# An MLP cut by inner width instead of by tokens, in a four-layer Mamba/FFT/convolution kernel

## The chip, the cores and the metric

The kernel runs on one core of one Trainium2 chip, in float32. The metric is the device time of one execution in microseconds (us); a lower one is better. A core has five engines that run side by side, each with its own queue of instructions: TensorE (PE in the profile; its weight loads are listed as PEld), VectorE (DVE), ScalarE (ACT), GpSimd (POOL) and SyncE (SP), which here issues all the DMAs.

## The reference, cut to what matters

The input is 8 images of 384 channels and 32 x 32 pixels, so 1024 tokens an image. Four layers follow each other, each added to its input: layer 0 is a Mamba block (inner width 768, 16 states), layer 1 an 8 x 8 patch FFT filter with a depthwise convolution and a gate, layer 2 a Mamba block with a layer norm ahead and an MLP behind, layer 3 a 3 x 3 depthwise convolution. The change touches only the MLP of layer 2:

```
# t: tokens x 384, the output of layer 2's Mamba block
t = gelu(t @ mlp_w1.T + mlp_b1, approximate=False) @ mlp_w2.T + mlp_b2
# mlp_w1: 1536 x 384, mlp_w2: 384 x 1536
x = x + t
```

## The kernel before, in words

Channels lie on the 128 partitions (KC = 3 blocks of 128), tokens on the free axis. An image is worked in NCH = 2 chunks of T = 512 tokens. Layers 0 and 1 run for all images first, then layers 2 and 3, joined by the intermediate x_mid in DRAM. So there are 16 chunks of layer 0 and 16 chunks of layer 2.

The backbone is the scan. A chunk has NQ = 24 steps. In a step t the program (the loop at line 1015) issues: the product with B on POOL for the next step (`times`, L623), the four scans on DVE (`scan`, L643, with two products with C on DVE, L654, and one on POOL, L660), filler, the reduction of the step before on TensorE (`gather`, the y matmuls), the load of the g tile three steps ahead (`begin`, L613), more filler, and the matmuls and exponentials of the next step's decay (`decay`, the dA matmuls and L241). The four dA banks of PSUM are single, so the dA matmuls of step t+1 come after DVE has read those of step t, and after all filler that stands ahead of them in TensorE's queue.

The filler is everything else: the projections in (ps_in) and of the gates (ps_z), the output projection (ps_out), the MLP (ps_up, ps_dn), layer 3 (ps_dw), norms and loads. Each is a Python generator, a job, which yields after each piece. `Jobs` hands out pieces while the step has room: it counts a matmul as its columns over 600 units and gives a step of layer 2 a room of 6.4 units of TensorE and 3.0 of VectorE (`ROOM`). A piece is let in when the remaining room is at least what the piece of the same number needed in the last job of its kind. Jobs go in the order of their due step `last`; unused room is carried over up to an eighth, and debt is carried over in full. `jobs.until` forces pieces without regard to room when a step needs their result. A job that yields NEXT goes on in the next step, one that yields EARLY at the start of the next step. `pipe` runs units of several stages through PSUM banks (`NBANK` = 3); with `deep=1` one unit at a time, one stage a piece, and the last stage of a unit shares its piece with the first of the next.

The MLP belongs to the job `finish(s)`: `out_proj` writes t into SBUF (three tiles of 128 x 512) and calls `weights()`; then `mlp(s)` runs. It goes over two halves of the tokens (TH = 256). In each half the up stage makes all NF = 12 blocks of the inner width: for a pair of blocks f, f+1 it takes one weight tile (128 x 6 x 128, 384 KB), puts 2 x 3 matmuls of 256 columns into the two halves of one bank, and ACT evicts the two halves with the bias into h1 (128 x 12 x 256). Then two gelus over 1536 columns each, then the down stage: for each of the 3 output blocks m two weight tiles and 12 matmuls of 256 columns, all 12 accumulated in PSUM, and one scalar_tensor_tensor on DVE that adds the sum and the bias b2 to x.

The weight tiles (tag mw) have 4 buffers. `weights()` lists the 12 tiles twice, once a half, and asks for the first four. `take()` asks for one more tile (`more()`, L889, on SP's queue) and hands out the oldest loaded. The request goes into the buffer of the tile just used up, so it waits for TensorE's last matmul of that tile. On SP's queue stand also the g loads (L613, 1 MB each, which wait for the y matmuls to free a buffer) and the spills of du (L590, four for each d, which wait for POOL).

A float32 matmul of the program is two TensorE instructions, each with a weight load, in the profile: 72 up matmuls a chunk x 16 chunks are 2304 instructions. All matmuls are issued on line 177, all activations on line 241; the tiles tell them apart.

Of the kernel before, what the change touches and what calls it, by code (L numbers as in the profile page):

```python
# [10 lines left out]
F32 = mybir.dt.float32  # L11
AF = mybir.ActivationFunctionType
ALU = mybir.AluOpType
# [3 lines left out]
P = 128  # L17
B, C, H, W = 8, 384, 32, 32
L = H * W
KC = C // P  # L20
# [6 lines left out]
T = 512  # L27
NCH = L // T
FF = 4 * C
NF = FF // P  # L30
# [23 lines left out]
def _flat(ap):  # L54
    return ap.rearrange("p a b -> p (a b)")
# [100 lines left out]
def tile_conv_preact_d4(ctx: ExitStack, tc: tile.TileContext, a: dict, out: bass.AP):  # L156
# [13 lines left out]
    vector = Meter(nc.vector, work, 1)  # L170

    def mm(out_, lhsT, rhs, start=True, stop=True):
        columns = 1
        for n in rhs.shape[1:]:
            columns *= n
        work[0] += columns / 600
        nc.tensor.matmul(out_, lhsT, rhs, start=start, stop=stop)  # L177
# [11 lines left out]
    def pipe(units, deep=2):  # L189


        flying = []
        units = deque(units)
        while units or flying:
            went = bool(flying)
            for f in list(flying):
                if f["stages"]:
                    f["stages"].popleft()(f["ps"])
                settle(f)
                if not f["stages"]:  # L200
                    flying.remove(f)
            if units and live["ps"] < NBANK and len(flying) < deep:
                went = True
                name, stages = units.popleft()
                live["ps"] += 1
                ps = psg.tile([P, 512], F32, tag="ps", name=name)
                stages[0](ps)
                f = {"stages": deque(stages[1:]), "ps": ps, "bank": True}
                settle(f)
                if f["stages"]:  # L210
                    flying.append(f)
            if units or flying:
                yield None if went else WAIT

    def settle(f):
        if f["bank"] and (not f["stages"] or f["stages"][0] is None):
            f["bank"] = False
            ps_done()
            if f["stages"]:
                f["stages"].popleft()  # L220

    def both(*stages):


        def run(ps):
            for stage in stages:
                stage(ps)

        return run
# [3 lines left out]
    def act(out_, in_, func, **kw):  # L233

        if func in (AF.Exp, AF.Ln):
            if act_set["now"] != "exp":
                nc.scalar.preload_act_table_set(SET_EXP)
                act_set["now"] = "exp"
        elif func not in (AF.Identity, AF.Copy, AF.Square, AF.Abs):
            act_set["now"] = func  # L240
        nc.scalar.activation(out_, in_, func, **kw)  # L241

    def exp_again():

        nc.scalar.preload_act_table_set(SET_EXP)
        act_set["now"] = "exp"

    def rsqrt(out_, in_, eps):
# [20 lines left out]
    ln_w, ln_b, b1, b2 = (  # L269
        vec2[:, 0:3], vec2[:, 3:6], vec2[:, 6 : 6 + NF], vec2[:, 18:21],  # L270
    )
# [414 lines left out]
    def out_proj(s):  # L686
# [6 lines left out]
        if last:  # L693
            while "done" not in chunks[B * NCH - 1]:
                yield WAIT
            if p2 is None:
                open_p2()
            s["weights"] = weights()
            s["t"] = [p2.tile([P, T], F32, tag="t", name="t", bufs=3) for _ in range(KC)]
# [22 lines left out]
    def finish(s):  # L722

        yield from out_proj(s)
        t = NQ * s["n"]
        if s["n"] == B * NCH - 1:
            load_out(layer_w["l2_"], "l2_")
        if s["pre"] == "l2_":
            yield from mlp(s)
        s["ended"] = True  # L730
        if s["pre"] == "l2_":
            if s["c"] == NCH - 1:
                jobs.add("layer3", layer3(s), 0, t + 3 * NQ - 1)
        elif s["c"] == NCH - 1:
            until = 2 * NQ + 3 if s["n"] == B * NCH - 1 else 3 * NQ - 2
            jobs.add("layer1", layer1(s), 0, t + until)

    p2 = None
# [120 lines left out]
        s["done"] = True  # L859


    TH = T // 2
    NFH = NF // 2
    xp = None

# [6 lines left out]

    def weights():

        parts = [a["l2_mlp_w1"][f : f + 2].rearrange("f p k q -> p f k q") for f in range(0, NF, 2)]
        parts += [
            a["l2_mlp_w2"][m][:, g * NFH : (g + 1) * NFH, :]
            for m in range(KC)
            for g in range(2)
        ]  # L880
        parts = deque(parts + parts)
        loaded = deque()

        def more():
            if parts:
                w = p2.tile([P, NFH, P], F32, tag="mw", name="mw", bufs=4)
                part = parts.popleft()
                to = w if len(part.shape) == 3 else w.rearrange("p (f k) q -> p f k q", f=2)
                nc.sync.dma_start(to, part)  # L889
                loaded.append(w)  # L890

        for _ in range(4):
            more()
        return loaded, more

    def mlp(s):
        x = s["x"]
        loaded, more = s["weights"]
        first = True

        def take():

            nonlocal first
            if not first:
                more()
            first = False
            return loaded.popleft()

        for half in range(2):
            cols = slice(half * TH, (half + 1) * TH)  # L910
            h1 = p2.tile([P, NF, TH], F32, tag="h1", name="h1")

            def up(f):
                def run(q):
                    def run_q(ps):
                        if q == 0:
                            now[0] = take()
                        cols_q = slice(q * TH, (q + 1) * TH)
                        for k in range(KC):
                            mm(  # L920
                                ps[:, cols_q], now[0][:, q * KC + k, :],
                                s["t"][k][:, cols], start=k == 0, stop=k == KC - 1,
                            )

                    return run_q

                def evict(ps):
                    for q in range(2):
                        act(
                            h1[:, f + q, :], ps[:, q * TH : (q + 1) * TH], AF.Identity,  # L930
                            bias=b1[:, f + q : f + q + 1],
                        )

                now = [None]
                return [run(0), both(run(1), evict)]

            yield from pipe([("ps_up", up(f)) for f in range(0, NF, 2)], deep=1)
            yield EARLY
            for q in range(2):
                part = _flat(h1[:, q * NFH : (q + 1) * NFH, :])  # L940
                act(part, part, AF.Gelu)
            exp_again()
            yield NEXT

            def down(m):
                def sum_up(g, third):
                    def run(ps):
                        if third == 0:
                            now[0] = take()
                        for f in range(third * KC, (third + 1) * KC):  # L950
                            mm(
                                ps[:, :TH], now[0][:, f, :], h1[:, g * NFH + f, :],
                                start=g == 0 and f == 0, stop=g == 1 and f == NFH - 1,
                            )

                    return run

                now = [None]

                def add(ps):  # L960
                    xc = x[:, m, cols]
                    vector.scalar_tensor_tensor(
                        xc, ps[:, :TH], b2[:, m : m + 1], xc, ALU.add, ALU.add
                    )

                return [sum_up(0, 0), sum_up(0, 1), sum_up(1, 0), both(sum_up(1, 1), add)]

            yield from pipe([("ps_dn", down(m)) for m in range(KC)], deep=1)

    def layer3(s):  # L970
# [44 lines left out]
    for t in range(total):  # L1015
        s, i = steps[t]
# [16 lines left out]
        if t > 0:  # L1033
            p, q = steps[t - 1]
# [4 lines left out]
        if t + AHEAD < total:  # L1039
            p, q = steps[t + AHEAD]  # L1040
# [138 lines left out]
```

## Time and profile before

| | |
|---|---|
| three runs | 7766.74, 7783.18, 7798.79 us; median 7783.18 |
| profiled execution | 7774.96 us; span 7773.2 us; 1.8 us around it |
| mean granted TensorE clock | 0.922 |
| scans of layer 2 with their filler | about 4068 to 7600 us |
| tail without scans (last out projection, MLP, layer 3) | about 7600 to 7773 us |
| mw loads | 384 of 384 KB; 7.4 us from issue to landing in the median, 16.2 at most |
| all DMA | 1122.5 MB, 144 GB/s over the span |

The groups of instructions that the change touches (count, busy us, mean ns of one):

| group | count | busy us | mean ns |
|---|---|---|---|
| PE ps_up, 256 columns | 2304 | 566.8 | 394 |
| PE ps_dn, 256 columns | 2304 | 573.9 | 401 |
| ACT eviction h<-ps_up, 128 x 256 | 384 | 158.4 | 474 |
| ACT gelu of h, 128 x 1536 | 64 | 91.4 | 1476 |
| DVE x<-ps_dn, 128 x 256 | 96 | 45.3 | 472 |

How to read it: the mean of a matmul is its own length from first to last column out; matmuls of a group overlap, so their pace is read from starts in the timeline, not from the mean. "idle before, releaser" is the time an engine stood still ahead of an instruction, and the event that ended it. SPq is SP's queue of DMAs.

### The profile page before, as it was taken

The page shows a single profiled execution, that of the slowest core. Times are in us where ns is not written, and L with a number is a line of the kernel's source. Part 1 is how long each engine was busy: PE and PEld are TensorE (multiplying, and loading weights), DVE is VectorE, ACT ScalarE, POOL GpSimd, SP SyncE. Part 2 cuts the span into 40 slices and gives each one's busy share as a digit, 9 for nine tenths or more (in the row PEclk, how much of TensorE's full clock was granted, in tenths as well). Part 3 has the DMA queues.
Part 4 walks back from the last instruction along what each step waited for, and adds up shares of the span by engine and source line. Part 5 has one row for each costly group of instructions (what it writes and reads, how often), then busy time and mean ns, then how long its engine had stood idle before and what let it go on. Part 6 is the DMA issues. An engine that isn't in the chain of part 4 may idle for free. (4 is left out here: it accounts for less than half of the span.)

```text
span 7773.2 us, 76689 instructions
## 1 busy us (share of the span) xinstructions
PE 7244.1 (93%) x25762; PEld 3001.0 (39%) x25762; DVE 5787.0 (74%) x7350; ACT 4034.0 (52%) x6980; POOL 5638.8 (73%) x2710
## 2 busy tenths in 40 slices
PE   7989999999999999999999989999999999999998
PEld 2223333333333333333334434444444444444445
DVE  5988788888777878778746765767777677776871
ACT  4445555554554555455545544555555555555543
POOL 5888878788787878778646764767767677676770
PEclk8888889999888999988899999999999999999999
DMA  5666556556565646556536654666656666565662
GB/s 141 141 151 144 138 134 142 136 135 150 127 146 127 141 120 148 128 139 146 129 78 167 174 135 120 165 156 172 165 150 174 155 170 164 149 164 146 171 168 67
DMA packets 288919, 1122.50 MB, mean 144 GB/s; under 512 B 37386, under 2 KB 90970, under 8 KB 190220
## 3 DMA queue, kind: packets, MB, share of 16 engines
q1 hardware_dynamic: 288524, 1117.59, 58.4%
q8 instruction: 204, 3.34, 0.2%
q14 instruction: 191, 1.56, 0.1%
HBM read 1041.96 MB, written 75.50 MB: 144 GB/s over the span
## 5 line engine op out<-in xcount | busy, mean ns | idle before, releaser
L623 POOL TENSOR_TENSOR g<-g,bc 128x1024 f32<-128x1024 f32 x1536 | 3586.8, 2358 | 197.2 <-DMA g<-dud 181.2
L660 POOL TENSOR_TENSOR g<-g,bc 128x1024 f32<-128x1024 f32 x768 | 1806.2, 2352 | 1441.1 <-DVE carry L656 806.6
L241 ACT ACTIVATE dA<-dA,w_A 128x512 f32<-128x512 f32 x3072 | 1860.7, 662 | 1543.3 <-PE dA L177 1530.1
L177 PE MATMUL dA<-dt,selr 32*128 32x512 f32 x6144 | 1573.3, 677 | 70.6 <-DVE g L654 61.9
L643 DVE TENSOR_TENSOR_SCAN dA<-dA,carry,g 128x512 f32<-128x512 f32 x768 | 986.6, 1285 | 616.0 <-issue 275.6
L643 DVE TENSOR_TENSOR_SCAN dA<-dA,g 128x512 f32<-128x512 f32 x768 | 940.6, 1225 | 477.5 <-issue 167.7
L654 DVE TENSOR_TENSOR g<-dA,bc 128x512 f32<-128x512 f32 x1536 | 1053.9, 686 | 29.8 <-DVE dA L643 0.5
L177 PE MATMUL y<-g,sely 128*32 128x512 f32 x6144 | 934.1, 637 | 43.0 <-POOL g L660 37.5
L643 DVE TENSOR_TENSOR_SCAN g<-dA,carry,g 128x512 f32<-128x512 f32 x768 | 940.6, 1267 | 0.0
L643 DVE TENSOR_TENSOR_SCAN g<-dA,g 128x512 f32<-128x512 f32 x768 | 893.3, 1204 | 0.0
L177 PEld LDWEIGHTS dA<-dt,selr 32*128 32x128 f32 x6144 | 470.2, 191 | 984.4 <-DVE g L643 517.3
L177 PE MATMUL ps_dn<-h,mw 128*128 128x256 f32 x2304 | 573.9, 401 | 75.3 <-DMA mw<-in_l_mlp_w 58.6
L177 PE MATMUL ps_up<-t,mw 128*128 128x256 f32 x2304 | 566.8, 394 | 59.0 <-DMA mw<-in_l_mlp_w 44.2
L177 PE MATMUL ps_z<-xf,w_in 128*128 128x512 f32 x1152 | 586.1, 649 | 27.3 <-DVE dt L85 23.6
L177 PE MATMUL ps_in<-xf,w_in 128*128 128x512 f32 x1152 | 566.9, 633 | 27.3 <-DVE u L85 25.5
L177 PE MATMUL ps_dw<-tp,diag 96*96 96x512 f32 x1152 | 572.8, 638 | 15.2 <-ACT diag L241 15.2
L177 PE MATMUL ps_out<-u,w_out 128*128 128x512 f32 x1152 | 543.7, 619 | 10.2 <-DVE x L85 10.2
L177 PEld LDWEIGHTS ps_dn<-h,mw 128*128 128x128 f32 x2304 | 439.5, 197 | 277.0 <-issue 118.8
L177 PEld LDWEIGHTS ps_up<-t,mw 128*128 128x128 f32 x2304 | 425.8, 192 | 268.4 <-issue 148.9
L177 PE MATMUL ps_dw<-xp,diag 128*128 128x512 f32 x864 | 407.5, 622 | 42.2 <-ACT diag L241 40.9
L241 ACT ACTIVATE u<-ps_in,w_vec 128x512 f32<-128x512 f32 x192 | 149.4, 778 | 484.2 <-PE ps_in L177 484.2
L177 PEld LDWEIGHTS y<-g,sely 128*32 128x32 f32 x6144 | 134.2, 111 | 648.5 <-issue 461.1
(99 smaller groups left out, 6463.1 us busy)
## 6 DMA issues: line engine op xcount, KB each, us to landing
g<-dud SPq DMA_DIRECT2D x768, 1024.0 KB, 7.1
mw<-in_l_mlp_w SPq DMA_DIRECT2D x384, 384.0 KB, 7.4
dud<-du SPq DMA_DIRECT2D x768, 64.0 KB, 1.7
xk<-in_x SPq DMA_DIRECT2D x48, 256.0 KB, 4.2
xf<-in_x SPq DMA_DIRECT2D x16, 768.0 KB, 8.4
x<-in_x SPq DMA_DIRECT2D x16, 768.0 KB, 8.5
x_mid<-x SPq DMA_DIRECT2D x16, 768.0 KB, 4.6
xk<-x_mid SPq DMA_DIRECT2D x48, 256.0 KB, 5.0
```

The costliest lines, as they stand in the source:

```text
L177: nc.tensor.matmul(out_, lhsT, rhs, start=start, stop=stop)
L241: nc.scalar.activation(out_, in_, func, **kw)
L623: nc.gpsimd.tensor_mul(g, g, s["bc"][:, 0, :].unsqueeze(1).to_broadcast([P, 2, T]))
L643: nc.vector.tensor_tensor_scan(dAs[j] if j < own else g[:, j, :], dAs[j], g[:, j, :], 0.0 if s["c"] == 0 else carry[:, q : q + 1], ALU.mul ...
L654: nc.vector.tensor_mul(g[:, j, :], dAs[j], s["bc"][:, 1, :])
L660: nc.gpsimd.tensor_mul(g, g, s["bc"][:, 1, :].unsqueeze(1).to_broadcast([P, 4 - own, T]))
```

## The change

The two passes of the MLP are now two parts of the inner width, each for all 512 tokens of the chunk. Part g makes blocks 6g to 6g+5: up matmuls of 512 columns, one bank and one eviction a block, h1 is 128 x 6 x 512 (the same size). Then two gelus of 1536 columns, then for each m one weight tile and 6 matmuls of 512 columns. The partial sum of part 0 is added to x with the bias by scalar_tensor_tensor, that of part 1 by tensor_add. `weights()` lists each tile once, in the order of use: three tiles of W1 and three of W2 for part 0, then the same for part 1. A stage of `pipe` is now one matmul: a unit of the up stage has three, one of the down stage six.

```diff
     def weights():

-        parts = [a["l2_mlp_w1"][f : f + 2].rearrange("f p k q -> p f k q") for f in range(0, NF, 2)]
-        parts += [
-            a["l2_mlp_w2"][m][:, g * NFH : (g + 1) * NFH, :]
-            for m in range(KC)
-            for g in range(2)
-        ]
-        parts = deque(parts + parts)
+        parts = deque()
+        for g in range(2):
+            for f in range(g * NFH, (g + 1) * NFH, 2):
+                parts.append(a["l2_mlp_w1"][f : f + 2].rearrange("f p k q -> p f k q"))
+            for m in range(KC):
+                parts.append(a["l2_mlp_w2"][m][:, g * NFH : (g + 1) * NFH, :])
         loaded = deque()
...
     def mlp(s):
         x = s["x"]
         loaded, more = s["weights"]
-        first = True
+        now = [None]

         def take():

-            nonlocal first
-            if not first:
+            if now[0] is not None:
                 more()
-            first = False
-            return loaded.popleft()
-
-        for half in range(2):
-            cols = slice(half * TH, (half + 1) * TH)
-            h1 = p2.tile([P, NF, TH], F32, tag="h1", name="h1")
+            now[0] = loaded.popleft()
+
+        for g in range(2):
+            h1 = p2.tile([P, NFH, T], F32, tag="h1", name="h1")

             def up(f):
-                def run(q):
-                    def run_q(ps):
-                        if q == 0:
-                            now[0] = take()
-                        cols_q = slice(q * TH, (q + 1) * TH)
-                        for k in range(KC):
-                            mm(
-                                ps[:, cols_q], now[0][:, q * KC + k, :],
-                                s["t"][k][:, cols], start=k == 0, stop=k == KC - 1,
-                            )
-
-                    return run_q
+                def run(k):
+                    def run_k(ps):
+                        if f % 2 == 0 and k == 0:
+                            take()
+                        mm(
+                            ps, now[0][:, f % 2 * KC + k, :], s["t"][k], start=k == 0,
+                            stop=k == KC - 1,
+                        )
+
+                    return run_k

                 def evict(ps):
-                    for q in range(2):
-                        act(
-                            h1[:, f + q, :], ps[:, q * TH : (q + 1) * TH], AF.Identity,
-                            bias=b1[:, f + q : f + q + 1],
-                        )
-
-                now = [None]
-                return [run(0), both(run(1), evict)]
-
-            yield from pipe([("ps_up", up(f)) for f in range(0, NF, 2)], deep=1)
+                    act(
+                        h1[:, f, :], ps, AF.Identity,
+                        bias=b1[:, g * NFH + f : g * NFH + f + 1],
+                    )
+
+                return [run(0), run(1), both(run(2), evict)]
+
+            yield from pipe([("ps_up", up(f)) for f in range(NFH)], deep=1)
             yield EARLY
             for q in range(2):
-                part = _flat(h1[:, q * NFH : (q + 1) * NFH, :])
+                part = _flat(h1[:, q * KC : (q + 1) * KC, :])
                 act(part, part, AF.Gelu)
             exp_again()
             yield NEXT

             def down(m):
-                def sum_up(g, third):
+                def sum_up(f):
                     def run(ps):
-                        if third == 0:
-                            now[0] = take()
-                        for f in range(third * KC, (third + 1) * KC):
-                            mm(
-                                ps[:, :TH], now[0][:, f, :], h1[:, g * NFH + f, :],
-                                start=g == 0 and f == 0, stop=g == 1 and f == NFH - 1,
-                            )
+                        if f == 0:
+                            take()
+                        mm(ps, now[0][:, f, :], h1[:, f, :], start=f == 0, stop=f == NFH - 1)

                     return run

-                now = [None]
-
                 def add(ps):
-                    xc = x[:, m, cols]
-                    vector.scalar_tensor_tensor(
-                        xc, ps[:, :TH], b2[:, m : m + 1], xc, ALU.add, ALU.add
-                    )
-
-                return [sum_up(0, 0), sum_up(0, 1), sum_up(1, 0), both(sum_up(1, 1), add)]
+                    xm = x[:, m, :]
+                    if g == 0:
+                        vector.scalar_tensor_tensor(
+                            xm, ps, b2[:, m : m + 1], xm, ALU.add, ALU.add
+                        )
+                    else:
+                        vector.tensor_add(xm, ps, xm)
+
+                return [sum_up(f) for f in range(NFH - 1)] + [both(sum_up(NFH - 1), add)]

             yield from pipe([("ps_dn", down(m)) for m in range(KC)], deep=1)
```

More of the change, by code (lines that the diff above doesn't have):

```diff
@@ L859, in layer1 @@
         s["done"] = True
-    TH = T // 2
     NFH = NF // 2
```

## The prediction, made before the changed kernel was run

> **What bounds the kernel now.** I read the page's busy times first, then stretches, then the waits of TensorE.
>
> ```profile
> PE 7244.1 (93%) x25762; PEld 3001.0 (39%) x25762; DVE 5787.0 (74%) x7350; ACT 4034.0 (52%) x6980; POOL 5638.8 (73%) x2710
> ```
>
> TensorE (PE) leads, but this is a mean. The MLP tiles are first used at 4068 us, so the change can only act after that. The busy times by stretch, split there, at 4850 and at the last scan:
>
> ```profile
> core 0: us, PE busy (x) PEld busy (x) DVE busy (x) ACT busy (x) POOL busy (x), PEclk, DMA share, GB/s
> 4068.00:4850.00 782.00, 709.28 (x2663) 343.04 (x2662) 519.17 (x684) 386.19 (x632) 488.64 (x239) 0.93 0.58 147
> 4850.00:7600.00 2750.00, 2576.96 (x10210) 1229.45 (x10209) 2047.07 (x2596) 1486.07 (x2473) 1986.57 (x945) 0.96 0.64 161
> 7600.00:7773.00 173.00, 151.57 (x490) 97.37 (x488) 12.24 (x23) 53.01 (x110) 0.78 (x4) 0.92 0.23 72
> ```
>
> PE is busy 94% of the middle stretch, with DVE at 74% and POOL at 72%. Over the 3705 us PE idles 3705 - 3438 = 267 us. Who ended that idle time, from the list of waits on PE for 4068 to the end (us in total, times, longest):
>
> ```profile
> PE ps_dn L177 <- DMA mw<-in_l_mlp_w: 58.6, 24, 5.6
> PE ps_up L177 <- DMA mw<-in_l_mlp_w: 44.2, 34, 4.8
> PE ps_dw L177 <- ACT diag L241: 40.9, 16, 4.6
> PE ps_lv L177 <- ACT sq L241: 34.4, 12, 3.0
> PE ps_in L177 <- DVE u L85: 17.8, 27, 3.8
> ```
>
> Waiting for MLP weights is the largest cause: 58.6 + 44.2 = 102.8 us in 58 waits. Waits of dA for DVE, the sign of a scan that sets the pace, are not near the head, so PE sets it. One such step on PE's timeline:
>
> ```profile
> 5854.57 1.07 PE L177 MATMUL y<-g,sely 128*32 128x512 f32 x8
> 5855.56 1.56 PE L177 MATMUL ps_dn<-h,mw 128*128 128x256 f32 x6
> 5858.92 1.56 PE L177 MATMUL ps_dn<-h,mw 128*128 128x256 f32 x6 [1.79 <-DMA mw<-in_l_mlp_w]
> 5860.41 1.14 PE L177 MATMUL dA<-dt,selr 32*128 32x512 f32 x8
> ```
>
> The dA matmuls start the next scan and are queued behind the waiting ps_dn. On the same timeline DVE's last scan of the step ended at 5857.97, so dA, at 5860.41, was late by the 1.79 us and not by DVE. I did this for all 51 steps that hold such a wait: the idle time before dA that DVE would have allowed adds up to 102.4 of the 102.9 us found. The waits are on the path.
>
> Why a tile is late: its queue.
>
> ```profile
> 5853.43 1.74 SPq L590 DMA_DIRECT2D dud<-du  x4
> 5855.27 0.37 SPq L889 DMA_DIRECT2D mw<-in_l_mlp_w  x1
> 5855.76 0.52 SPq L613 DMA_DIRECT2D g<-dud  x1
> 5856.37 0.54 SPq L889 DMA_DIRECT2D mw<-in_l_mlp_w  x1
> ```
>
> The weights share SP's queue with the spill of du, which waits for POOL, and with the g load, which waits for y. Landing takes 7.4 us in the median and 16.2 at most (issues of tile mw). A tile is requested when the tile three places before it begins: with 256 columns three tiles are 3 x 12 PE instructions x 0.217 us = 7.8 us of PE time.
>
> **What the Trainium skill says.** "TensorE: Matmul & The Clock Gate", section "What's actually happening": after an idle window of about 3.4 us the array runs at half clock until a busy one has passed. The trace agrees: in the tail 72 ps_dn after an idle 3.72 us take 18.65 us, 72 ps_up without it 15.79:
>
> ```profile
> 7612.57 15.61 PE L177 MATMUL ps_out<-u,w_out 128*128 128x512 f32 x36
> 7628.02 15.79 PE L177 MATMUL ps_up<-t,mw 128*128 128x256 f32 x72
> 7647.54 18.65 PE L177 MATMUL ps_dn<-h,mw 128*128 128x256 f32 x72 [3.72 <-ACT h L241]
> ```
>
> Same page, section "LDWEIGHTS (loading the stationary operand)": a load costs its columns over 1.2 GHz, 107 ns for 128. Here an f32 load takes 190 ns, and the measurement decides; it is still under the pitch of 217 ns, so halving the loads frees nothing by itself. "DMA: Bandwidth & Descriptors", section "Issuing engines are not separate DMA queues": all DMAs interleave on the same 16 engines, so g and mw slow each other. DMA is at 0.64 in the middle stretch, so neither saturates it; that fewer mw loads make g land sooner no run here shows yet.
>
> **The change part by part.**
> - Loads: 384 become 192, 75.5 MB less of 1122.5 MB, and SP is spared 192 x 0.396 us = 76 us of issue. Each tile now feeds 12 PE instructions of 512 columns, 12 x 0.429 us = 5.15 us, so the lead is 15.4 us of PE time. PE's own y and dA stand between (1.07 + 1.14 us of a step; the step shown takes 10.55 us from dA to dA, 8.8 without its wait), so it is about 20 us of clock against 7.4 median and 16.2 worst. Up to one step (9 us) in SP's queue still leaves the median covered. **Waits: -102.8; I keep 8 us for rare ones (0 to 30).**
> - Half clock: the clock column loses 0.07 x 782 + 0.04 x 2750 + 0.08 x 173 = 179 us, twice that at half speed (340 us by the unrounded records). In 44 us of it the largest PE idle just before was a weight wait. Half speed loses half, 22 us at most; other idle stands near several of them. **-12 (0 to -22).**
> - Matmuls: 4608 instructions of 256 columns become 2304 of 512. From the tail, 36 ps_out start 15.45 us before the next group (429 ns each), and 72 ps_up fill 15.55 to 15.64 us in the chain (216 to 217 ns). 4608 x 0.2165 = 998; 2304 x 0.429 = 988. **-8 (0 to -12).**
> - Adds on DVE: 96 of 472 ns (45 us) become 48 scalar_tensor_tensor and 48 tensor_add of 512 columns. The rows of the same forms out of PSUM are 744 (y) and 678 ns (x<-ps_out): 68 us. +23 us on an engine at 74%, hidden by PE. **0**; +23 if DVE became the bound; the very last add costs 0.2.
> - Evictions on ACT: 384 of 474 ns become 192 of 594 (the z row): about 68 us less by the sum of durations, on an engine at 54% that PE outlasts. **0** (0 to -5). Gelus and table loads keep their number and size.
> - Order: the up stage goes in steps of one matmul, the down stage too, so the planner fits smaller pieces (0.85 and 1.7 of its units of 600 columns instead of 1.28 and 2.56) into a step's room of 6.4. The total work stays, and PE is the bound inside and outside the steps, so moving it costs **0** (-10 to +30). On SP the W2 tiles of the first part move ahead of the second part's W1 tiles: the pop order is the same as the load order, nothing waits longer. A mw load that waits for PE to free its buffer still holds up a g load behind it, half as often (318 us of such waits on SP before).
> - Next late: once PE waits less, POOL is next. In a step with a du it has 2.35 (L660) + 2 x 2.36 (L623) + 1.27 (L583) = 8.3 us against PE's 8.8. It fits, barely; **+10 (0 to 50)** for steps where it doesn't.
>
> Sum: -102.8 + 8 - 12 - 8 + 10 = -105 us. Against the profiled execution (7774.96 us, span 7773.2, 1.8 around it) that is 7670; the median of the runs, 7783.18, lies 8 above it, so **7678**.
>
> **Rivals.**
> - **The gain is half lost to POOL and DVE.** For it: 8.3 against 8.8 us in the du steps, and POOL waits 76 us for g in the middle stretch. Against: du falls in 6 of 24 steps of a chunk, and g loads face fewer others. Half of 103, and the half-clock gain gone: -48, so 7735. Chance 0.15.
> - **More than the waits.** If denser steps also end part of the other 300 us at half clock (many begin where only y, dA and small matmuls run), 100 us fewer give 50 us: -155, so 7628. Against: those causes stay. Chance 0.11.
> - **The steps run dry: slower.** Smaller pieces fill each step, so layer 3's matmuls, the filler, are used up early; then DVE's scan chain sets the pace while PE idles. Before, one step per image takes 35.16 us because 60 ps_dw and 12 ps_z are forced into it (30.7 units, 24 more than the room): that is the reserve. I count about 6 MLP steps per image that hold 5.12 units and could hold 6.4: 7.7 units absorbed, far under 24. Slower needs 24 + 105/8 = 37 or more per image, at 1.0 us a unit; 45 would give 21 x 8 = 168 - 105 = +63, so 7846. Chance 0.06.
> - That the loads are not halved is excluded: the queue of parts is no longer doubled, and the pops match it, 12 a chunk.
>
> **How the numbers follow.** The forecast (7648 to 7705) has 0.68. The range, 7625 to 7742, adds most of the first rival and half of the second. What this measurement can tell from no change is 0.5%, 39 us: faster is below 7744. Faster: 0.68 + 0.11 + 0.12 of the first rival = 0.91; the same 0.03 + 0.01 = 0.04; slower 0.05.
>
> **What would show it.** 192 mw loads. PE's waits for mw at 10 us or less in place of 103; if they stay over 40, the lead was not the cause. 72 ps_up instructions in the tail near 30.9 us. Half clock after the start of layer 2 at 315 to 340 us. If PE's waits for mw go but the span falls under 60 us, look at dA's waits for DVE and at POOL's for g; if those grow, the first rival holds. If PE idles in steps with few pieces and the 35 us step has vanished, it is the third. I would be wrong most of all if half clock grew: it is the one cost I took from records without a rule for it.

## The result, and the profile after

The changed kernel takes 7798.79 us in the median of 20 runs (7780.91 to 7822.83), the kernel before 7788.78 in 20 runs beside them (7746.60 to 7805.42). The ratio is 1.0016, with a 95% interval of 1.0005 to 1.0026. So nothing was gained: the weights are loaded half as often, and the kernel is the same within half a per cent, if anything 0.16% slower. The profiled execution has a span of 7800.5 us at a mean granted clock of 0.914 (before 7773.2 at 0.922). 7678 was forecast.

From the page of the changed kernel, its busy times and the issues of the weight tiles (count, size, median us from issue to landing):

```profile
PE 7237.9 (93%) x23458; PEld 2566.8 (33%) x23458; DVE 5820.7 (75%) x7350; ACT 4004.4 (51%) x6788; POOL 5632.9 (72%) x2710
...
mw<-in_l_mlp_w SPq DMA_DIRECT2D x192, 384.0 KB, 7.1
```

TensorE has 2304 instructions fewer and the 192 loads are there, but its busy time fell by only 6.2 us. The stretches of the changed kernel, split at the same places in its work as before (columns as there: stretch, its length, busy time of PE, PEld, DVE, ACT and POOL with their instructions, PE's clock, DMA share, GB/s):

```profile
4087.00:4880.00 793.00, 739.07 (x2368) 263.47 (x2367) 564.32 (x747) 410.04 (x638) 529.78 (x258) 0.93 0.54 135
4880.00:7620.00 2740.00, 2516.89 (x8320) 897.46 (x8319) 2036.31 (x2531) 1431.21 (x2277) 1939.12 (x924) 0.94 0.56 139
7620.00:7800.00 180.00, 157.31 (x369) 70.26 (x367) 15.99 (x27) 55.17 (x107) 3.13 (x5) 0.94 0.13 44
```

The split is the first ps_up: layer 2's scans begin some 520 us earlier, its MLP begins here. It lies 18 us later than before (4087 against 4068). The program up to there is the same, and ten profiled executions of kernels of this document reach it between 4068 and 4098 us (the kernel with the loads alone, below, at 4098): that is a difference of executions, not of the change. From there to the end it is 3713 us, 8 more than the 3705 before. TensorE idles 3713 - 3413 = 300 us of them, where it idled 267; and the clock column loses 0.07 x 793 + 0.06 x 2740 + 0.06 x 180 = 231 us, where it lost 179. Both have grown. Who ended the idle time, from the list of waits on PE from 4068 us to the end (us in total, times, longest):

```profile
PE ps_in L177 <- DVE u L85: 54.0, 28, 4.9
...
PE ps_dt L177 <- ACT bc L241: 40.1, 6, 6.8
...
PE ps_up L177 <- DVE dt L85: 25.7, 7, 4.2
PE ps_up L177 <- ACT h L241: 23.7, 12, 3.0
```

The two waits for mw, 102.8 us, are gone altogether. In their place ps_in waits for DVE with 54.0 us where it had 17.8, ps_dt for bc with 40.1 where it had 0.7, and ps_up for dt with 25.7 (5.5) and for h with 23.7 (5.4). Two more of ps_up are new: 12.5 us for u, and 15.7 that the profile puts down to nothing. Together these six grew by 36.2 + 39.4 + 20.2 + 18.3 + 12.5 + 15.7 = 142 us; smaller ones fell by a few. No load is among them. In the program ps_in reads no u, ps_dt no bc and ps_up none of dt, h and u: these tiles are written by the instructions that read an earlier matmul's sum out of a bank. So five of the six are waits for a place in PSUM; the next views show it for ps_in.

The loss lies at a place that comes back in every second chunk in the later half of layer 2: the steps with the input projection of the next chunk. They stand here for the changed kernel and then for the kernel before (columns as above):

```profile
5986.80:6086.40 99.60, 75.51 (x222) 25.05 (x218) 56.39 (x60) 41.96 (x64) 55.63 (x24) 0.83 0.37 88
```

```profile
5976.00:6057.00 81.00, 76.92 (x316) 36.10 (x314) 69.56 (x75) 52.06 (x85) 61.10 (x27) 0.98 0.59 143
```

In the changed kernel this stretch goes from the start of one dA group to the start of the seventh after it: 7 steps in 99.6 us, 14.2 us a step. In the kernel before it holds nine steps (72 dA instructions, eight to a step) in 81.0 us, 9.0 us a step. Both have the same 36 ps_in instructions in it. TensorE is busy for 76% of the time at a clock of 0.83, where it was busy for 95% at 0.98. PE's timeline of the changed kernel at this place (start, length, group; in brackets the idle time ahead and what ended it):

```profile
5964.20 2.84 PE L177 MATMUL ps_dw<-xp,diag 128*128 128x512 f32 x6
...
5976.59 2.84 PE L177 MATMUL ps_dw<-xp,diag 128*128 128x512 f32 x6
...
5998.75 2.81 PE L177 MATMUL ps_in<-xf,w_in 128*128 128x512 f32 x6 [0.67 <-DVE u L85]
...
6006.73 5.46 PE L177 MATMUL ps_in<-xf,w_in 128*128 128x512 f32 x6 [4.17 <-DVE u L85]
...
6015.25 1.14 PE L177 MATMUL dA<-dt,selr 32*128 32x512 f32 x8
...
6082.76 3.68 PE L177 MATMUL ps_dw<-xp,diag 128*128 128x512 f32 x6
```

DVE's timeline at the same place:

```profile
6002.71 2.45 DVE L643 TENSOR_TENSOR_SCAN g<-dA,carry,g 128x512 f32<-128x512 f32 x2
6005.07 1.51 DVE L85 SCALAR_TENSOR_TENSOR u<-ps_in,w_vec,u 128x511 f32<-128x511 f32 x2
```

The ps_in group of 5998.75 is done at 6001.6. The next one waits from 6002.6 until DVE's two taps of the first (the u instructions, which read ps_in out of PSUM) end at 6006.6: they stand in DVE's queue behind the four scans of the step. One group of ps_in waits for the reading of the one before it only when both use the same bank. Then it runs at half clock, 5.46 us in place of 2.81, and the dA matmuls of the next step, behind it, come at 6015.25. The kernel before at the same work:

```profile
5997.92 2.84 PE L177 MATMUL ps_in<-xf,w_in 128*128 128x512 f32 x6
6001.69 2.84 PE L177 MATMUL ps_in<-xf,w_in 128*128 128x512 f32 x6
6006.03 2.81 PE L177 MATMUL ps_in<-xf,w_in 128*128 128x512 f32 x6 [0.40 <-DVE u L85]
```

There the second follows without a wait and the third after 0.4 us. The built programs say the same: counting the chunks of both Mamba layers from 0, the six ps_in of chunk 22 go to banks 0, 2, 0, 2, 0, 2 in the kernel before and all six to bank 2 in the changed one, and again in chunks 24, 26, 28 and 30. These ps_in stand among the scans of the chunk before, so among those of chunks 21, 23, 25, 27 and 29.

Who holds another bank is in the same view. A sum of layer 3 is three ps_dw groups of six; this one has its first at 5964.20, its second at 5976.59 and its third only at 6082.76, and DVE first reads it at 6086.47 (acc, the only one in these 130 us). It keeps a bank for over 120 us, while all six ps_in pass. That it was begun here comes from the sizes of the pieces. An up piece is now 0.85 units where it was 1.28, a down piece 0.85 where it was 1.28 too, and the planner's room comes out differently: in the step of 5964.20 a norm's matmuls have taken 2.56 units, the out projection's next piece of 5.12 doesn't fit into what is left, and the first piece of layer 3's sum (2.56) does; the kernel before has a group of ps_out there. After that other jobs are due earlier than layer 3, and its sum stands. The third bank belongs to the up unit in work, which keeps it between its pieces. That is not new: in the kernel before an up unit holds one bank during the ps_in of all these chunks too, and two are left. New is that layer 3's sum holds another at the same time. So one bank of three is left to ps_in, ps_bc and ps_dt.

### The profile page after: what moved, and what is told of

Its sections match the earlier page's. It is cut to its first block, busy times and chain, and to the rows that moved or that the text cites. A ratio compares the mean times of both kernels' runs of the same rounds, so it can differ in the third digit from the quotient of the medians.

```text
span 7800.5 us, 71430 instructions
## 1 busy us (share of the span) xinstructions
PE 7237.9 (93%) x23458; PEld 2566.8 (33%) x23458; DVE 5820.7 (75%) x7350; ACT 4004.4 (51%) x6788; POOL 5632.9 (72%) x2710
## 5 line engine op out<-in xcount | busy, mean ns | idle before, releaser
L660 POOL TENSOR_TENSOR g<-g,bc 128x1024 f32<-128x1024 f32 x768 | 1804.2, 2349 | 1527.3 <-DVE g L643 748.1
L177 PE MATMUL dA<-dt,selr 32*128 32x512 f32 x6144 | 1536.0, 678 | 78.8 <-DVE g L654 69.9
L177 PEld LDWEIGHTS dA<-dt,selr 32*128 32x128 f32 x6144 | 454.1, 192 | 1044.0 <-DVE g L643 484.6
L177 PE MATMUL ps_up<-t,mw 128*128 128x512 f32 x1152 | 589.1, 643 | 80.1 <-DVE dt L85 25.7
L177 PE MATMUL ps_dn<-h,mw 128*128 128x512 f32 x1152 | 550.6, 619 | 14.2 <-ACT h L241 12.4
L85 DVE SCALAR_TENSOR_TENSOR u<-ps_in,w_vec,u 128x511 f32<-128x511 f32 (+1 forms) x384 | 282.6, 744 | 151.3 <-ACT xt L241 126.3
L177 PEld LDWEIGHTS ps_up<-t,mw 128*128 128x128 f32 x1152 | 218.4, 202 | 434.1 <-issue 332.3
```

The lines of the kernel that those rows point to most:

```text
L85: return call(out_, *args, **kw)
L660: nc.gpsimd.tensor_mul(g, g, s["bc"][:, 1, :].unsqueeze(1).to_broadcast([P, 4 - own, T]))
```

## The experiments

All ratios are to the kernel before in the same session, with a 95% interval. "Idle" and "half clock" count TensorE's idle time and its time at half clock from the first ps_up to the end of a profiled execution, from the unrounded records.

**The loads alone.** The kernel before with its old pieces, but only every second tile of its list is loaded, and each loaded tile serves two uses in turn. So there are 192 loads; half of the weights are left out, and half of the products are made with a tile that isn't theirs. The number and the size of the instructions on TensorE stay.

```diff
-        parts = deque(parts + parts)
+        parts = deque((parts + parts)[::2])
...
-            nonlocal first
-            if not first:
-                more()
-            first = False
-            return loaded.popleft()
+            nonlocal taken, tile_
+            if taken % 2 == 0:
+                if taken:
+                    more()
+                tile_ = loaded.popleft()
+            taken += 1
+            return tile_
```

> The kernel before with its own order of work, but only every second weight tile of its list is loaded and each loaded tile is used for two sets in a row (192 loads, lead doubled; half the products are made with the wrong weights, so the MLP's values are not the reference's). Theory (the weight waits were on the path and nothing takes their place in the old order): TensorE's waits for mw fall from 103 us to under 15, the span falls by 95 to 125 us, about 7660 to 7690. Rival (the waits are covered by POOL, DVE or the clock, so taking them away gains little in any order): within 30 us of the kernel before.

Measured: 7701.25 us, ratio 0.9886 (0.9873 to 0.9899), 88 us less than 7788.95 and a little less than expected. The head of PE's list of waits in this kernel:

```profile
PE ps_dw L177 <- ACT diag L241: 40.9, 16, 4.6
...
PE ps_up L177 <- DVE dt L85: 27.8, 11, 3.6
```

All mw waits are gone; ps_up behind dt has grown (5.5 to 27.8), and ps_in behind u has not (18.0). So the waits for weights were on the path, as the prediction had it, and the step that priced them was sound. Landing falls to 3.9 us in the median here. What follows is that something else in the change costs as much again.

**The pieces alone.** The kernel before, with its 384 loads and its matmuls of 256 columns, cut into pieces as the change cuts them: three to an up unit, six to a down unit, of the same size in units.

```diff
-                        cols_q = slice(q * TH, (q + 1) * TH)
-                        for k in range(KC):
+                        for j in (2 * q, 2 * q + 1):
+                            k, h = j % KC, j // KC
+                            cols_q = slice(h * TH, (h + 1) * TH)
...
-                return [run(0), both(run(1), evict)]
+                return [run(0), run(1), both(run(2), evict)]
...
-                        for f in range(third * KC, (third + 1) * KC):
+                        for f in range(part % 3 * 2, part % 3 * 2 + 2):
...
-                return [sum_up(0, 0), sum_up(0, 1), sum_up(1, 0), both(sum_up(1, 1), add)]
+                return [sum_up(i) for i in range(5)] + [both(sum_up(5), add)]
```

> The kernel before with its token halves and 384 loads, but its stages cut to two matmuls of 256 columns, so that the planner sees pieces of the same size as in the changed kernel and gives the same order and the same banks. Theory (two separate effects): the bank waits of the changed kernel come on top of the weight waits, 80 to 130 us slower than before, 7860 to 7910, with ps_in<-DVE u near 50 us and mw waits at 60 to 105. Rival (the loss comes from loading once or from the 512 columns): within 30 us of the kernel before.

Measured: 7940.65 us, ratio 1.0195 (1.0182 to 1.0208), 152 us more, above what was expected. The head of its list of waits on PE:

```profile
PE ps_dn L177 <- DMA mw<-in_l_mlp_w: 67.0, 33, 4.9
PE ps_in L177 <- DVE u L85: 54.0, 28, 4.9
PE ps_up L177 <- DMA mw<-in_l_mlp_w: 44.3, 28, 3.5
...
PE ps_dt L177 <- ACT bc L241: 40.0, 6, 6.8
```

The waits of the changed kernel are here to 0.1 us (54.0 in 28, 40.0 in 6), on top of those for weights. This kernel and the changed one give TensorE the same groups in the same order, and its ps_in go to the same banks. So neither the wider matmuls nor the adds on DVE nor the evictions make these waits: the cut into pieces does. Half clock, which the expectation did not count, rose too: 514 us against 340 before.

**Layer 3 kept out of the banks.** The changed kernel, but layer 3's sum may not open a bank while a chunk's norm and input projection are in work.

```diff
         if s["pre"] == "l2_":
+            live["in"] = True
             yield from layer_norm(xn)
...
+            live["in"] = False
             yield WAIT
+        live["in"] = s["pre"] == "l2_"
...
         yield from pipe([("ps_bc", [spread(j)]) for j in range(2)])
+        live["in"] = False
...
             if t == 0:
+                while live["in"]:
+                    yield WAIT
                 ps = yield from ps_tile("ps_dw")
```

> The changed kernel, but layer 3 takes no new PSUM bank while a chunk of layer 2 is between its layer norm and its ps_bc. Theory (with the new pieces layer 3's depthwise sum starts one step before the ps_in matmuls, is left hanging with a bank, the MLP's up unit holds another, so all six ps_in of every second chunk go through one bank and each waits for DVE to read it): the waits ps_in<-DVE u (54 us), ps_dt<-ACT bc (40 us), ps_up<-ACT h and ps_up<-DVE (78 us) fall to under 60 together, half clock after 4068 us falls from 445 to 350 us or less, the span by 80 to 130 us, about 7670 to 7720. Rival (the finer pieces or the 512 columns cost the time by themselves, through the clock): within 30 us of the changed kernel.

Measured: 7769.96 us, ratio 0.9984 (0.9968 to 1.0001): 29 us below the changed kernel and far from the gain expected. From the list of its waits on PE, the head and the wait in question:

```profile
PE ps_up L177 <- DVE dt L85: 34.4, 11, 5.8
...
PE ps_in L177 <- DVE u L85: 3.0, 13, 0.3
```

The wait of ps_in for u has fallen from 54 to 3 us, and idle from 297 to 241 us: without layer 3's hold that wait is gone. But ps_up waits longer (34.4 us for dt, 29.1 for u, 28.1 for h), and layer 3's work, put off, is forced in elsewhere: one step takes 75.0 us, and its chunk 299 us, where most take 233 to 258.

The time from the first dA group of a chunk to that of the next shows how both add up. The scans of chunks 21, 23, 25, 27 and 29 take 222 to 224 us each with the loads alone, 258 to 261 in the changed kernel, and 233 to 242 here. So the five lost 181 us to the new pieces at equal loads, and the hold of layer 3 accounts for about half of it, 96 us. The one long chunk and the other chunks give most of that back. In the changed kernel itself something was also won: in chunk 20 a step of 65.9 us became one of 32.3, since the MLP's matmuls are no longer forced into it, and the chunk takes 60 us less than with the loads alone. The 98 us between the two kernels are what is left of a loss nearly twice as large. The bank theory stands for the wait; that freeing this bank would bring the loss back falls.

**Units in one piece.** The changed kernel with an up unit as one piece (2.56 units) and a down unit as two (2.56 each), so that no up unit holds a bank between pieces. Layer 3's sum may hold one as before. The second kernel here has only the first of the two edits.

```diff
-                return [run(0), run(1), both(run(2), evict)]
+                return [both(run(0), run(1), run(2), evict)]
...
-                return [sum_up(f) for f in range(NFH - 1)] + [both(sum_up(NFH - 1), add)]
+                return [
+                    both(*(sum_up(f) for f in range(KC))),
+                    both(*(sum_up(f) for f in range(KC, NFH)), add),
+                ]
```

> The changed kernel with coarser stages: an up unit is one stage of three matmuls, a down unit two stages of three, so an up unit holds its bank only within one piece and the ps_in go round all three banks. Theory: no weight waits and no one-bank chunks, 7640 to 7700. Rival (any order other than before's costs about 100 us): 7760 to 7810.

> The changed kernel with only the up unit made one stage of three matmuls, the down unit left at six: the up unit no longer holds a bank between pieces, layer 3's sum may still hold one, so ps_in go through two banks. Theory (it takes two idle holders to leave one bank): ps_in<-DVE u falls from 54 to under 20 us, ps_up<-ACT h from 39 to under 10, PE's idle time after the first ps_up from 297 to 200 to 240 us; 7740 to 7780, since steps of 5.12 units come back as in e4. Rival (layer 3's held bank alone does the harm): ps_in<-DVE u stays over 40 us and the time within 20 us of the changed kernel.

Measured: 7757.39 us, ratio 0.9951 (0.9937 to 0.9965), with both edits, and 7780.11, ratio 0.9989 (0.9976 to 1.0001), with the first alone. With both edits no wait of ps_in for u is in the list any more; with the first alone it stands at

```profile
PE ps_in L177 <- DVE u L85: 4.4, 11, 0.4
```

In the program of this second kernel layer 3's sum still holds a bank while the ps_in of chunks 22, 24, 26, 28 and 30 pass, and they take turns in the two others. So it takes both holders to make the wait, and without either of them it is gone. Idle falls from 297 us to 186 and 193. But of some 105 us of idle that went, 41 and 19 came off the time: with both edits the time lies 57 us above the expected range, next to the rival's; with the first alone it is within the 20 us of its rival, though the wait which that rival rests on, over 40 us, isn't there. TensorE's busy time says where it went. The dA lines of the page, for the changed kernel and for that with both edits:

```profile
L177 PE MATMUL dA<-dt,selr 32*128 32x512 f32 x6144 | 1536.0, 678 | 78.8 <-DVE g L654 69.9
```

```profile
L177 PE MATMUL dA<-dt,selr 32*128 32x512 f32 x6144 | 1630.6, 675 | 86.5 <-DVE g L654 76.5
```

The same 6144 instructions are busy for 95 us more, at the same mean length of one. The four dA banks are single, so dA matmuls follow DVE's reading bank by bank; where DVE sets the pace they come out one by one, and a group reaches over more time without an idle gap that the list of waits would show. This happens in steps that hold two pieces of 2.56: 5.12 of a room of 6.4, since a third does not fit. What is left undone is forced in at one place. PE's timeline of the kernel with both edits there:

```profile
6141.72 15.72 PE L177 MATMUL ps_dn<-h,mw 128*128 128x512 f32 x36
6157.28 15.62 PE L177 MATMUL ps_dw<-xp,diag 128*128 128x512 f32 x36
```

This one step lasts 57.8 us. It holds 126 filler instructions, 53.8 units, where the changed kernel has 25.6 units at the same place (the 58.9 of the next expectation is too high), and DVE, whose scans are the backbone, does no scan in most of it. So TensorE is not the bound in every step: steps with too little filler wait for the scans, and the work they didn't take comes back where the scans wait for TensorE.

**Room for three.** If that is so, a room of 6.8, which lets a third piece of 2.56 in every second step or so, must help the coarse pieces. That three fit rests on a slack that the description of `Jobs` above leaves out: the program lets a piece in when the room is within 0.1 of what it needs. With the carry of an eighth a step begins with 7.65, and 2.53 are left after two pieces. This is the kernel with both edits and

```diff
-ROOM = {"l0_": (5.2, 3.0), "turn": (6.4, 3.0), "l2_": (6.4, 3.0)}
+ROOM = {"l0_": (5.2, 3.0), "turn": (6.4, 3.0), "l2_": (6.8, 3.0)}
```

> The changed kernel with the coarse stages of e4 and a room of 6.8 instead of 6.4 units a step in layer 2. Theory (e4 lost its gain because pieces of 2.56 units leave 1.28 of 6.4 unused, so most steps hold 5.12 units, wait for the scan chain, and the rest piles up in steps of 58.9 units and the tail, where DVE idles): three pieces fit into about every second step, the pile-ups go, the dA and y matmuls fall from 567 + 379 us back to about 520 + 352, and it is faster than e4 by 40 us or more: 7660 to 7720. Rival (the order of filler is worth nothing, TensorE sets the pace anyway): within 20 us of e4, 7740 to 7775.

Measured: 7598.49 us, ratio 0.9757 (0.9737 to 0.9777), 189 us below the kernel before at 7787.52, better than expected, and the fastest of all. Its PE timeline, dA groups and filler:

```profile
6046.33 1.78 PE L177 MATMUL dA<-dt,selr 32*128 32x512 f32 x8
...
6051.81 5.42 PE L177 MATMUL ps_dw<-xp,diag 128*128 128x512 f32 x12
6057.16 1.14 PE L177 MATMUL dA<-dt,selr 32*128 32x512 f32 x8
...
6064.77 1.67 PE L177 MATMUL dA<-dt,selr 32*128 32x512 f32 x8
```

A step with three pieces (6046.33 to 6057.16, 10.8 us) and one with two (to 6064.77, 7.6 us) take turns. After two pieces the dA group is drawn out to 1.67 and 1.78 us: TensorE arrives just as DVE frees the banks. After three it takes 1.14: TensorE is the later one. dA is busy for 1527.3 us in the whole kernel.

**The room alone.** The same line in the kernel before, all else as it was.

> The kernel before with a room of 6.8 instead of 6.4 in layer 2, nothing else: a control for e5b. Theory (the old pieces of 1.28 and 2.56 with 6.4 already fill the steps, and more MLP work a step drains the weights faster): 7780 to 7850, waits for mw at 103 us or more. Rival (the room alone is what e5b gains): 7680 to 7740.

Measured: 7872.7 us, ratio 1.0116 (1.0095 to 1.0137), 85 us slower. Its list begins:

```profile
PE ps_dn L177 <- DMA mw<-in_l_mlp_w: 73.8, 30, 5.3
PE ps_up L177 <- DMA mw<-in_l_mlp_w: 49.2, 23, 5.1
```

A larger room is no gain of itself: the waits for weights grow to 123 us, idle to 328 and half clock to 467.

**The best order with the old loads.** The kernel before, 384 loads and 256 columns, with the coarse pieces and the room of 6.8.

```diff
-ROOM = {"l0_": (5.2, 3.0), "turn": (6.4, 3.0), "l2_": (6.4, 3.0)}
+ROOM = {"l0_": (5.2, 3.0), "turn": (6.4, 3.0), "l2_": (6.8, 3.0)}
...
-                return [run(0), both(run(1), evict)]
+                return [both(run(0), run(1), evict)]
...
-                return [sum_up(0, 0), sum_up(0, 1), sum_up(1, 0), both(sum_up(1, 1), add)]
+                return [
+                    both(sum_up(0, 0), sum_up(0, 1)),
+                    both(sum_up(1, 0), sum_up(1, 1), add),
+                ]
```

> The kernel before (token halves, 384 loads, 256 columns) in the order of e5b: an up unit is one stage of 1.28 + 1.28 units, a down unit two stages of 2.56, and the room in layer 2 is 6.8. The matmul groups stand in the same order and in the same banks as in e5b, only the loads and the columns differ. Theory (halving the loads is worth 90 to 150 us in any order, the order is worth the rest): waits for mw of 90 to 150 us, 7690 to 7760. Rival (the good order alone makes e5b, the loads no longer matter there): within 25 us of e5b, 7575 to 7625.

Measured: 7800.41 us, ratio 1.0020 (1.0009 to 1.0030), so slower than expected. PE's list begins:

```profile
PE ps_dn L177 <- DMA mw<-in_l_mlp_w: 72.9, 24, 6.9
PE ps_up L177 <- DMA mw<-in_l_mlp_w: 55.5, 22, 4.1
```

The fastest order is worth nothing while the weights come late. The three orders with both numbers of loads, in us (medians):

| order of the pieces | 384 loads | 192 loads | loads halved |
|---|---|---|---|
| as before | 7789 | 7701 | -88 |
| single matmuls, as the change has it | 7941 | 7799 | -142 |
| whole units, room 6.8 | 7800 | 7598 | -202 |

In the two lower rows the right column also has the 512-column matmuls and the adds. In each row the order of TensorE's groups is the same on both sides. On the left 103, 111 and 128 us of waits for weights stand in the list, on the right none, and the profiles show how this comes to such different sums:

| row | span from first ps_up | idle | half clock while busy | idle + half of the half clock |
|---|---|---|---|---|
| as before | -88 | -79 | +1 | -78 |
| single matmuls | -148 | -96 | -74 | -133 |
| whole units, room 6.8 | -188 | -132 | -120 | -192 |

At half clock six ps_in took 5.46 us above, at full clock 2.81: about half of the time at half clock is lost, so half of that column counts. The last column accounts for the second to within 15 us. In the first row the waits cost less than their sum, since others grew in their place and half clock stayed; in the two lower rows they cost more, and the surplus goes with the half clock. That the waits for weights took the clock down there is likely and not shown.

## Why the prediction was wrong, step by step

- **Loads and their waits: right.** 192 loads; of 102.8 us of waits none is left, where 8 were kept. Landing takes 7.1 us in the median and 11.1 at most, inside the lead that was worked out. The g loads land no sooner than before (7.1 us in the median, both times), which answers what the prediction left open. Alone, in the old order, they are worth 88 us (0.9886).
- **Matmuls and adds: right.** In the tail of the changed kernel a part's 36 ps_up take 15.61 us, so both parts 31.2, forecast at 30.9; the 144 of 256 columns took 2 x 15.79. (The working's 998 less 988 is 10, where 8 was entered.) The adds on DVE take 741 and 676 ns, forecast at 744 and 678, and are hidden.
- **Evictions: too cheap, without effect.** One of 512 columns with bias takes 686 ns, not the 594 of the z row. By the sum of durations, as the prediction counted, that is 182 to 132 us, so 50 less on ACT and not 68; by busy time 158.4 to 131.1, 27 less.
- **Order: this is the step that failed.** "The total work stays, and PE is the bound inside and outside the steps, so moving it costs 0 (-10 to +30)." At 192 loads the old order takes 7701 us and the new one 7799: moving the work cost 98 where 0 was put, and at 384 loads it cost 152. The working looked at how much fits into a step, and neither at how long a piece keeps its bank nor at who takes the last one; and PE is not the bound in every step, as the coarse pieces show. The profile of before had a hint: ps_in waited for u 27 times already (17.8 us). A third of it, 5.8 us, fell on chunk 20, where in the program of before layer 3's sum and an up unit hold two banks together during three of the six ps_in.
- **Half clock: the sign was wrong.** -12 was forecast, with 315 to 340 us at half clock as the mark; it rose from 340 to 445. With the loads alone it stayed at 345, so taking the waits for weights away did not lower it in the old order; with the new order it rose (514 with the pieces alone). The danger was named ("most of all if half clock grew"), but not priced.
- **Next late:** POOL at +10 was the guess. It was PSUM: from the first ps_up on y waited for POOL 0.6 us in all (before: not at all). No rival named PSUM. The steps didn't run dry either, as the third rival had it: dA's waits for DVE are 5.2 us (before 2.6), and the forced step is still there. It lost 5.1 of its 30.7 units (7.7 were estimated; the rival needs more than 24) and takes 30.0 us. A form of that rival does decide in the kernel with coarse pieces.

The sum, from the first ps_up on: idle +33, half clock while busy +44 and so +22, all the rest of TensorE's busy time -46 (dA drawn out less, ps_dn shorter, ps_up longer), together +9; measured are 3704.7 to 3713.6. The medians differ by 10.

**What stays open.** No run changes the clock alone, so how much of the half clock is an effect of the idle time, and how much comes of small matmuls with nothing beside them, isn't separated. That layer 3's sum and an up unit hold the two banks is read from the built programs and shown by the two kernels that take one or the other away; both also change the filling of the steps. The other half of what the five chunks lost isn't traced to single waits. How the 105 us of idle time of those kernels divide between drawn-out dA and forced steps was read from the profile, not tried by itself.

## What to carry to other kernels

When a change cuts a job into other pieces, price the order too: for each piece ask how long it now holds a buffer that other jobs share, and which piece newly fits where. Test a change that does two things as two kernels: here the gain of one (-88 us) and the loss of the other (+98 at 192 loads) hid each other completely. And read the waits together with the clock and with the busy time of groups whose work didn't change: a wait can vanish from the list and come back as a longer busy group.

## What the runs showed of the hardware

- **A wait can cost more than itself.** After 4.17 us of idle time six ps_in took 5.46 us where six take 2.81. "TensorE: Matmul & The Clock Gate", section "What's actually happening", in the Trainium skill, gives about one idle window of 3.4 us for the fall to half clock, and the trace agrees here: its clock record falls at 6005.97, 3.4 us after TensorE's last matmul ended at 6002.56. It isn't so for every wait: with the loads alone 103 us of waits went, and 88 us came off the time.
- **Half clock goes with idle time, but not in proportion.** Idle and half clock of the kernels, in us: fastest 170 and 279; loads alone 185 and 345; units in one piece 186 and 340; up unit alone in one piece 193 and 412; layer 3 kept out 241 and 395; before 264 and 340; changed 297 and 445; best order with the old loads 302 and 433; before with a larger room 328 and 467; pieces alone 393 and 514. With idle down from 264 (before) to 185 (loads alone) half clock did not fall, so the sum of idle time doesn't settle it.
- **Busy time of single-bank matmuls is no measure of their work.** dA's 6144 instructions, each 675 to 683 ns long in the mean, are busy for 1520 to 1631 us in these kernels.
